# A scan block's residual: from an add on VectorE to a matmul on TensorE and a copy on ScalarE

## The chip, the cores and the metric

The kernel runs on one core of one Trainium2 chip. The metric is device time in microseconds (us): the median of the runs of one launch that computes the whole function.

## What is computed

The function is a chain of four blocks on x of shape (4, 512, 256), with a context of shape (4, 64, 192): a cross attention with a feed-forward part, a transformer block (self attention, cross attention, gated feed-forward part), four layers of a selective scan (Mamba), and a second transformer block. All is float32. The change lies in the scan layers:

```python
h = jnp.concatenate([p, x], axis=1)          # p: 64 tokens made of the context
for l in range(L_):                          # 4 layers
    h = h + mamba_block(rmsnorm(h, norm_w[l]), ...)

def mamba_block(x, ...):
    xi, z = split(einsum('bsd,ed->bse', x, ip_w))        # 512 channels each
    xi = silu(causal_conv4(xi) + cb)
    dt, Bm, Cm = split(einsum('bse,fe->bsf', xi, xp_w))
    dt = softplus(dt @ dtp_w.T + dtp_b)
    # for 16 states: state = exp(dt*A)*state + dt*B*xi ; y = sum(state*C)
    y = (ys + xi * Dp) * silu(z)
    return einsum('bse,de->bsd', y, op_w)                # the output projection
```

The residual is the `h +` of the loop: the output projection's result is added to h.

## The kernel before

The scan block is `layer2` (from line 1311). Its state `hT_res` holds h, transposed: 128 features on the partitions, in two chunks (DC = 2), for each of four batches 512 tokens. The work goes by **units**: a unit is one layer and one batch, 16 in all, in order. The 512 channels of a unit are four chunks of 128, treated as two pairs; for each pair there are 16 steps, so a unit has 32 steps, and a step carries two of the 16 states of one chunk.

The heart of a step i:

- **decay** (line 1636, ScalarE, recorded at line 1644): two exponentials of 128x512 into a PSUM tile `ps_dA`, of which there are two; it is issued one step ahead.
- **product** (line 1628, GpSimd, line 1632): `dBu` of 128x1022, issued two steps ahead; **begin** (line 1646) is a two-column copy by ScalarE into the same tile.
- **states** (line 1651, VectorE, line 1659): the scan over 128x1024, in place in `ps_dA`, or for every fourth step into the tile `hP`.
- **outputs_here** (VectorE, line 1666): the product with C into `hC`, for the three steps in four that did not go to `hP`; the fourth is multiplied by GpSimd (line 1670).
- **add_up** (line 1672, TensorE, line 1692): transposes of `hC` or `hP` that accumulate in the PSUM tile `ps_y`.

Beside these steps run generators, each of which issues a few instructions and yields; the loop (lines 1731 to 1797) advances all of them twice a step. The program's order is therefore written by the loop, and each engine runs its own instructions in that order. The generators are `front` (line 1368, normalisation, input projection, convolution and the x projection `ps_x` of a unit two ahead), `step` (line 1485, dt), `gate` (line 1527, the z projection: `ps_z`, copied to `zs` by ScalarE at line 1541), `gated` (line 1546, the end of a unit) and `tokens` (line 1578, the last layer's result turned back). They share two PSUM banks, taken and given back with `bank` and `done`; `need` makes a generator yield until one is free. At the 10th and 15th step of a unit `flush_silu` (line 1720) runs the pending SiLUs on ScalarE, with a table load before and one behind (lines 1723 and 1644).

`gated` runs for a pair two steps after the pair's last. For the second pair its work falls into the first steps of the next unit: it transposes the gated output `g` (line 1559), copies it to `gT` (ScalarE, line 1562), and then, for each feature chunk c of two, makes the output projection `ps_out` of four matmuls of 128x512 (by `in_halves`, line 174, which yields once in the middle; its matmuls are recorded at line 178), yields three times, and adds the residual on VectorE at line 1574. In the instruction order that add stands between a step's scan and its product with C.

Of the kernel before, what the change touches and what calls it, by code (L numbers as in the profile page):

```python
# [15 lines left out]
P = 128  # L16
# [12 lines left out]
EC = E // P  # L29
# [95 lines left out]
def kernel(ctx: ExitStack, tc: tile.TileContext, t: dict, out: bass.AP):  # L125
    nc = tc.nc

    keep = ctx.enter_context(tc.tile_pool(name="keep", bufs=1))
    ident = keep.tile([P, P], F32, name="ident")
# [20 lines left out]
    def load_w(pool, name, shape, p=P, src=None, **kw):  # L150
        w = pool.tile(shape, F32, name=f"w_{name}", **kw)
        nc.sync.dma_start(out=w, in_=(t[name] if src is None else src).rearrange("(c p) n -> p c n", p=p))
        return w
# [20 lines left out]
    def in_halves(dst, pairs):  # L174

        h = len(pairs) // 2
        for i, (l, r) in enumerate(pairs):
            nc.tensor.matmul(dst, l, r, start=(i == 0), stop=(i == len(pairs) - 1))  # L178
            if i == h - 1:
                yield  # L180
# [1116 lines left out]
    def load_l1(wp, n):  # L1297
        if n in ("Wk2", "Wv2"):
            return load_w(wp, f"L1_{n}", [CP, 2, FF], CP, tag="w8")
        if n in ("Wo1", "Wo2", "Wf"):  # L1300
            return load_w(wp, f"L1_{n}", [P, FF // P, D], tag="w8")
        if n in ("Wpa", "Wpg"):
            half = 0 if n == "Wpa" else FF
            return load_w(wp, f"L1_{n}", [P, DC, FF], src=t["L1_Wp"][:, half : half + FF], tag="w8")
        return load_w(wp, f"L1_{n}", [P, DC, FF], tag="w8")
# [5 lines left out]
    def layer2(hT, A, far, h63, tail, X, fw, wl, late):  # L1311
# [5 lines left out]
        with ExitStack() as st:  # L1317
# [14 lines left out]
            def bank(name="m"):  # L1332
                k = banks.pop(0)
                tl = psum.tile([P, T], F32, name=f"ps_{name}", tag=f"m{k}", bufs=1)
                held[id(tl)] = k, tl
                return tl
# [3 lines left out]
            def need(n, rank):  # L1340

                me = (rank, n)
                while len(banks) < n + sum(k for r, k in wants if r < rank):
                    if me not in wants:
                        wants.append(me)
                    yield
                if me in wants:
                    wants.remove(me)

            def done(*tiles):  # L1350
                banks.extend(held.pop(id(tl))[0] for tl in tiles)
# [194 lines left out]
            def gated(n, pair):  # L1546

                l, b = divmod(n, B)
                q = units[n]
                w, g, gT = q["w"], q["g"], q["gT"]  # L1550
                if b == 0 and pair == 0:
                    w["out"] = load_w(wl, "out", [P, EC, D], src=t["L2_out"][l], tag="out")
                yield
                yield
                for i in range(2):
                    yield from need(1, 2)
                    ps = bank("gt")
                    for j in range(TPB):
                        nc.tensor.transpose(ps[:, j * P : (j + 1) * P], g[:, j, i * P : (i + 1) * P], ident)
                    yield  # L1560
                    yield
                    nc.scalar.copy(gT[:, 2 * pair + i, :], ps)
                    done(ps)
                if pair == 0:
                    return
                for c in range(DC):
                    yield from need(1, 2)
                    ps = bank("out")
                    yield from in_halves(ps, [(w["out"][:, m, c * P : (c + 1) * P], gT[:, m, :]) for m in range(EC)])
                    yield  # L1570
                    yield
                    yield
                    h = hT[:, c, b, :]
                    nc.vector.tensor_add(h, ps, h)
                    done(ps)
                q["done"] = True

# [152 lines left out]
            with tc.manual_schedule():  # L1730
                for i in range(first, last):
# [42 lines left out]
                    if closing:  # L1774
                        en, er = divmod(e - 1, US)
                        close_pair(en, er // PS)
                        active.insert(0, gated(en, er // PS))
# [143 lines left out]
    hT = hT_pool.tile([P, DC, B, T], F32, name="hT_res")  # L1921
# [36 lines left out]
    with ExitStack() as st:  # L1958
# [6 lines left out]
        w = {n: load_l1(wp, n) for n in ("Wq1", "Wk1", "Wv1", "Wo1")}  # L1965
# [89 lines left out]
```

## Time and profile before

| | |
|---|---|
| median of 3 runs | 4092.45 us (4090.92 to 4098.35) |
| the profiled execution | 4095.76 us |
| its span (first to last instruction) | 4093.9 us |
| mean granted TensorE clock | 0.910 |
| busy over the span: TensorE matmul, VectorE, ScalarE, GpSimd | 85%, 74%, 52%, 58% |
| scans on VectorE (line 1659) | 512, 877.1 + 291.8 us |
| products with C on VectorE (line 1666) | 384, 469.7 us |
| decays on ScalarE (line 1644) | 1024, 708.0 us |
| residual adds on VectorE (line 1574) | 32, 0.691 us each (median) |

A row of the profile names a line, an engine (PE is TensorE's matmul, PEld its weight load, DVE VectorE, ACT ScalarE, POOL GpSimd, SP SyncE), an operation, output and inputs, and shapes. In a timeline the columns are start, duration, and the group; in square brackets stands the idle time of the engine just before, and what ended it. TensorE's matmuls are pipelined, so that a row's duration overlaps the next row's.

### The profile page before, as it was taken

How to read it: one execution, taken by the hardware profiler on the slowest of the kernel's cores; microseconds unless marked ns; L12 is line 12 of the kernel's file. 1: busy time of each engine (PE TensorE's matmuls, PEld its weight loads, DVE VectorE, ACT ScalarE, POOL GpSimd, SP SyncE). 2: the span in 40 equal slices, each digit the busy share in tenths (PEclk: the TensorE clock that was granted, in tenths of full speed). 3: DMA queues.
4: the chain of work that ended last, by engine and by line, in shares of the span. 5: the costliest groups of instructions: out<-in, count | busy, mean ns of one | idle time of the engine just before them, and what ended most of it. 6: DMA issues, size and time to landing. Idle time of an engine off the chain costs nothing. (4 is left out here: it accounts for less than half of the span.)

```text
span 4093.9 us, 48583 instructions
## 1 busy us (share of the span) xinstructions
PE 3488.9 (85%) x17616; PEld 2194.8 (54%) x17616; DVE 3034.5 (74%) x2903; ACT 2148.5 (52%) x4366; POOL 2384.8 (58%) x1625
## 2 busy tenths in 40 slices
PE   7989998998888897887888788888887667999889
PEld 4654554554566554555555555555555444555446
DVE  5538567466465643899999999999999996676653
ACT  2345455354322433666667666666666553556422
POOL 2339259077100424899999999999998881000131
PEclk8999999999989998888888888888888678999999
DMA  2023123023100102444444445444444431000000
GB/s 76 11 81 101 32 76 101 18 87 105 45 1 0 57 27 84 150 160 156 155 166 155 161 153 168 160 160 146 170 160 145 151 130 37 1 1 1 1 6 16
DMA packets 140287, 369.93 MB, mean 90 GB/s; under 512 B 20624, under 2 KB 38224, under 8 KB 140048
## 3 DMA queue, kind: packets, MB, share of 16 engines
q1 hardware_dynamic: 136688, 363.58, 26.6%
q10 hardware_dynamic: 3360, 3.25, 0.3%
q8 instruction: 139, 2.28, 0.2%
q14 instruction: 100, 0.82, 0.1%
HBM read 363.50 MB, written 3.28 MB: 90 GB/s over the span
## 5 line engine op out<-in xcount | busy, mean ns | idle before, releaser
L1632 POOL TENSOR_TENSOR dBu<-dtx,bB 128x1022 f32<-128x1022 f32 x512 | 1199.9, 2364 | 47.6 <-DVE ps_dA L1659 47.5
L1644 ACT ACTIVATE ps_dA<-dt,A 128x512 f32<-128x512 f32 x1024 | 708.0, 691 | 471.9 <-DVE hC L1666 405.0
L1659 DVE TENSOR_TENSOR_SCAN ps_dA<-ps_dA,dBu 128x1024 f32<-128x1024 f32 x384 | 877.1, 2284 | 37.1 <-ACT ps_dA L1644 28.9
L1692 PE MATMUL ps_y<-ident,hC 128*128 128x128 f32 x3072 | 443.3, 295 | 89.9 <-DVE hC L1666 89.9
L1666 DVE TENSOR_TENSOR hC<-ps_dA,bC 128x1024 f32<-128x1024 f32 x384 | 469.7, 1223 | 24.4
L1692 PEld LDWEIGHTS ps_y<-ident,hC 128*128 128x128 f32 x3072 | 388.3, 153 | 175.0 <-DVE hC L1666 120.3
L967 ACT ACTIVATE pr<-ps_s,nm 128x512 f32<-128x512 f32 x512 | 344.8, 685 | 260.4 <-DVE nm L963 260.3
L963 DVE TENSOR_REDUCE nm<-ps_s 128x2 f32<-128x1024 f32 x256 | 301.4, 1218 | 157.8 <-PE ps_s L952 143.4
L981 PE MATMUL ps_pt<-ident,pr 128*128 128x128 f32 x2048 | 284.6, 279 | 69.1 <-DVE pT L986 31.4
L1670 POOL TENSOR_TENSOR hP<-hP,bC 128x1024 f32<-128x1024 f32 x128 | 302.0, 2359 | 54.9 <-ACT dBu L1649 21.1
L1659 DVE TENSOR_TENSOR_SCAN hP<-ps_dA,dBu 128x1024 f32<-128x1024 f32 x128 | 291.8, 2280 | 53.9 <-POOL dBu L1632 49.2
L981 PEld LDWEIGHTS ps_pt<-ident,pr 128*128 128x128 f32 x2048 | 232.0, 142 | 167.1 <-issue 61.4
L616 POOL TENSOR_TENSOR ln_rstd<-ln_rstd,const 128x4 f32<-128x4 f32 x24 | 24.4, 1017 | 437.7 <-DVE ln_rstd L615 436.1
L178 PE MATMUL ps_cv<-xp,w_dg 128*128 128x512 f32 x512 | 244.7, 615 | 35.2 <-ACT dBu L1649 28.6
L535 DVE TENSOR_TENSOR_SCAN phb<-pdA,phb 128x512 f32<-128x512 f32 x128 | 225.7, 1779 | 60.9 <-POOL phb L525 44.8
L984 ACT COPY pT<-ps_pt 128x512 f32<-128x512 f32 x256 | 140.4, 592 | 173.1 <-PE ps_pt L981 172.5
L1000 PE MATMUL ps_o<-pT,V 128*64 128x256 f32 (+1 forms) x2048 | 222.8, 394 | 1.8 <-ACT AT L1018 1.8
L1692 PE MATMUL ps_y<-ident,hP 128*128 128x128 f32 x1024 | 167.0, 317 | 66.5 <-POOL hP L1670 66.5
L952 PE MATMUL ps_s<-kT,qT 64*128 64x512 f32 (+1 forms) x1024 | 209.0, 646 | 2.2 <-DVE kT L1172 1.3
L525 POOL TENSOR_TENSOR phb<-hT_res,pm 128x512 f32<-128x512 f32 x128 | 188.1, 1474 | 35.8 <-DMA pm<-scrp 22.2
L1692 PEld LDWEIGHTS ps_y<-ident,hP 128*128 128x128 f32 x1024 | 145.8, 167 | 113.7 <-POOL hP L1670 72.3
L784 POOL TENSOR_TENSOR pr<-pr,rs 128x512 f32<-128x512 f32 x64 | 65.3, 1042 | 228.5 <-DVE rs L782 210.3
(276 smaller groups left out, 6372.4 us busy)
## 6 DMA issues: line engine op xcount, KB each, us to landing
bB<-scr SPq DMA_DIRECT2D x256, 512.0 KB, 3.7
bC<-scr SPq DMA_DIRECT2D x256, 512.0 KB, 4.1
pm<-scrp SPq DMA_DIRECT2D x224, 256.0 KB, 3.2
w_pw_in<-in_L_in SPq DMA_DIRECT2D x7, 512.0 KB, 4.5
X<-in_x SPq DMA_DIRECT2D x4, 512.0 KB, 7.4
w_L_W<-in_L_W SPq DMA_DIRECT2D x2, 1024.0 KB, 9.9
w_L_Wq<-in_L_Wq SPq DMA_DIRECT2D x2, 1024.0 KB, 6.3
w_L_Wo<-in_L_Wo SPq DMA_DIRECT2D x2, 1024.0 KB, 8.7
```

Of the source, the lines that this page charges most:

```text
L178: nc.tensor.matmul(dst, l, r, start=(i == 0), stop=(i == len(pairs) - 1))
L535: nc.vector.tensor_tensor_scan(hb, dA, hb, 0.0, ALU.mult, ALU.add)
L963: nc.vector.tensor_reduce(nm, ps, AX.X, ALU.max, negate=True)
L967: nc.scalar.activation(pr, ps[:, x, :], AF.Exp, bias=nm[:, x : x + 1], accum_out=rs[:, y : y + 1])
L981: nc.tensor.transpose(pp[:, t4, :], pr[:, t4 * P : (t4 + 1) * P], ident)
L1000: nc.tensor.matmul(ps_o[0][j * stride : (j + 1) * stride, half * W2 : (half + 1) * W2], Vs[n][0][:, t4, h * stride : (h + 1) * stride], pT ...
L1632: nc.gpsimd.tensor_mul(dBu[:, :, 1:], dtx[:, 1:].unsqueeze(1).broadcast_to([P, 2, T - 1]), bmap[i // 2, 0][:, :, 1:])
L1644: nc.scalar.activation(dA, dt, AF.Exp, scale=A[:, l, m, s : s + 1])
L1659: nc.vector.tensor_tensor_scan(to, dA, dBus.pop(i).rearrange("p s t -> p (s t)"), 0.0, ALU.mult, ALU.add)
L1666: nc.vector.tensor_mul(hCs[i], dA, bmap[i // 2, 1])
L1670: nc.gpsimd.tensor_mul(hCs[i], hCs[i], bmap[i // 2, 1])
L1692: nc.tensor.matmul(y[:, j, k * P : (k + 1) * P], hC[:, s, j * P : (j + 1) * P], ident, is_transpose=True, start=False, stop=(2 * s2 + s == ...
```

## The change

For each chunk c the residual h becomes the first matmul of the output projection's group: the identity as the stationary operand and h as the moving one, accumulated in the same PSUM bank as the four weight matmuls. The add on VectorE is replaced by a plain copy from PSUM to h on ScalarE. The list that `in_halves` gets now has five pairs, so its yield comes behind the second matmul (identity and first weight matmul) and three follow it; of the three yields before the result is taken, one is dropped.

```diff
                 for c in range(DC):
                     yield from need(1, 2)
                     ps = bank("out")
-                    yield from in_halves(ps, [(w["out"][:, m, c * P : (c + 1) * P], gT[:, m, :]) for m in range(EC)])
-                    yield
-                    yield
-                    yield
                     h = hT[:, c, b, :]
-                    nc.vector.tensor_add(h, ps, h)
+                    yield from in_halves(
+                        ps, [(ident, h)] + [(w["out"][:, m, c * P : (c + 1) * P], gT[:, m, :]) for m in range(EC)]
+                    )
+                    yield
+                    yield
+                    nc.scalar.copy(h, ps)
                     done(ps)
                 q["done"] = True
```

More of the change, by code (lines that the diff above doesn't have):

```diff
@@ L1568, in gated @@
                     ps = bank("out")
-                    yield from in_halves(ps, [(w["out"][:, m, c * P : (c + 1) * P], gT[:, m, :]) for m in range(EC)])
+                    h = hT[:, c, b, :]
+                    yield from in_halves(
+                        ps, [(ident, h)] + [(w["out"][:, m, c * P : (c + 1) * P], gT[:, m, :]) for m in range(EC)]
+                    )
                     yield
                     yield
-                    yield
-                    h = hT[:, c, b, :]
-                    nc.vector.tensor_add(h, ps, h)
+                    nc.scalar.copy(h, ps)
                     done(ps)
```

## The prediction

> **What bounds the kernel now.** I read four views in this order. First the busy time by stretch: the change touches only the scan block (about 1605 to 3397 us), so its balance of engines counts, not the page's averages. This is the row of one stretch in it, with its headings:
>
> ```profile
> core 0: us, PE busy (x) PEld busy (x) DVE busy (x) ACT busy (x) POOL busy (x), PEclk, DMA share, GB/s
> 2000.00:2500.00 500.00, 417.43 (x1944) 281.74 (x1944) 480.85 (x291) 341.46 (x625) 471.96 (x287) 0.86 0.46 160
> ```
>
> VectorE is busy 96% there, ScalarE 68%, TensorE 83%. By shares alone, taking work off VectorE is right. Second, what is taken, from the answer on line 1574 (min/median/max ns, then what ended VectorE's wait before it):
>
> ```profile
> L1574 DVE TENSOR_TENSOR hT_res<-ps_out,hT_res x32: 672/691/693, 1753.4 to 3396.3; 128x512 f32<-128x512 f32 x32
> ...
>   PE ps_out L178: 14.8, 9
> ```
>
> Third, where VectorE's missing 4% lies. I listed every pause of VectorE over 0.15 us in the 15 units that start inside the loop. All have one in common, about 7 us after the second residual add of a unit: 1.2 to 2.0 us long, and 0.2 us in the last, where one SiLU runs instead of two. In a plain unit (period 108.0 us from second add to second add) it is the only one. Fourth, therefore, the timelines of the three engines around it. VectorE:
>
> ```profile
> 2081.86 0.67 DVE L1574 TENSOR_TENSOR hT_res<-ps_out,hT_res 128x512 f32<-128x512 f32 x1
> 2082.44 1.21 DVE L1666 TENSOR_TENSOR hC<-ps_dA,bC 128x1024 f32<-128x1024 f32 x1
> 2083.57 2.28 DVE L1659 TENSOR_TENSOR_SCAN hP<-ps_dA,dBu 128x1024 f32<-128x1024 f32 x1
> ...
> 2087.98 0.69 DVE L1574 TENSOR_TENSOR hT_res<-ps_out,hT_res 128x512 f32<-128x512 f32 x1
> ...
> 2095.26 2.30 DVE L1659 TENSOR_TENSOR_SCAN ps_dA<-ps_dA,dBu 128x1024 f32<-128x1024 f32 x1 [2.00 <-ACT ps_dA L1644]
> ```
>
> ScalarE over the same time:
>
> ```profile
> 2085.89 1.42 ACT L1644 ACTIVATE ps_dA<-dt,A 128x512 f32<-128x512 f32 x2 [0.67 <-DVE hP L1659]
> 2087.24 0.18 ACT L1649 COPY dBu<-h 128x2 f32<-128x2 f32 x1
> 2087.42 1.28 ACT L1723 ACT_TABLE_LOAD   x1
> 2088.71 1.92 ACT L1723 ACTIVATE xi<-xi 128x2048 f32<-128x2048 f32 x1
> 2090.53 1.89 ACT L1723 ACTIVATE zs<-zs 128x2048 f32<-128x2048 f32 x1
> 2092.45 1.28 ACT L1644 ACT_TABLE_LOAD   x1
> 2093.74 1.42 ACT L1644 ACTIVATE ps_dA<-dt,A 128x512 f32<-128x512 f32 x2
> ```
>
> From 2085.89 to 2095.16 ScalarE never rests: decays, table load, two SiLUs, table load, decays. The scan at 2095.26 starts 0.10 us after the last decay. So at this one place per unit ScalarE, not VectorE, sets the pace: whatever makes the SiLU block start later moves that scan by the same amount, and VectorE has no other pause in a plain unit in which to win it back. TensorE:
>
> ```profile
> 2075.72 1.88 PE L185 MATMUL ps_z<-w_inz,hn 128*128 128x512 f32 x4
> 2077.44 3.60 PE L178 MATMUL ps_out<-gT,w_out 128*128 128x512 f32 x8
> 2080.88 1.88 PE L185 MATMUL ps_z<-w_inz,hn 128*128 128x512 f32 x4
> 2082.59 1.04 PE L1692 MATMUL ps_y<-ident,hP 128*128 128x128 f32 x8
> 2083.47 1.04 PE L1692 MATMUL ps_y<-ident,hC 128*128 128x128 f32 x8
> 2084.34 3.60 PE L178 MATMUL ps_out<-gT,w_out 128*128 128x512 f32 x8
> 2087.78 1.91 PE L1692 MATMUL ps_y<-ident,hC 128*128 128x128 f32 x16
> ```
>
> No idle is noted on any of these rows: TensorE has a queue of work here and the second ps_out is ready at 2087.94, 0.04 us before VectorE takes it, and 0.52 us after ScalarE has already begun its SiLU block. The page's chain of waits starts only near 3401 us and says nothing of the scan.
>
> **The change, part by part.** The order of the two programs' instructions, compared per engine, shows: VectorE loses 32 adds and nothing else moves; GpSimd and SyncE (all DMA issues) are unchanged; TensorE gets 32 identity matmuls, and in each unit's second group the identity and the first weight matmul now stand ahead of the 16 ps_y transposes behind which all four weight matmuls stood; ScalarE gets 32 copies. Each copy stands one half step earlier than the add did: the first (c = 0) ahead of the decays that ran at 2079.78, the second (c = 1) ahead of the decays that ran at 2085.89.
>
> Removed: 32 x 0.691 = 22.1 us of VectorE, 30 of these in the loop. In a plain unit their time is given back to the 2.00 us pause, since the scan behind it waits for ScalarE; I count them at nothing there and carry them through the timeline below.
>
> Added on TensorE: a 128x512 f32 matmul is two rows in the trace, started 0.429 us apart (eight rows of a group from 2077.44 on), so an identity matmul is 0.86 us. Two come before the second group's end: +1.72 us, because the queue is full. [...]
>
> Added on ScalarE: the copy of a 128x512 f32 PSUM tile. The nearest row is the gT copy (line 1562), 0.58 us. The price is small; the wait is not. The copy waits for TensorE, and behind it in ScalarE's queue stand a dBu copy, two decays and the SiLU block. [...] The profile's order agrees so far (decays and copies start in program order everywhere), but no row here isolates a ready instruction that was passed or not. If it did pass, the copy would cost at most 0.58[...].
>
> Now one plain unit, in the times of these rows. First copy: ps_out ready at 2081.04 + 0.86 = 2081.90; copy to 2082.52; a 1-column copy, two decays (1.42) to 2083.97; the scan of 2083.57 starts at 2084.07, although without the add it could have started 0.6 earlier. Its successor's decays end by 2085.9, in time. Second copy: ps_out ready at 2087.94 + 1.72 = 2089.66; copy to 2090.28; decays to 2091.72; dBu copy; SiLU block from 2091.84 instead of 2087.42. From there the same 7.84 us to the scan: 2099.68 instead of 2095.26, **+4.42 us**. VectorE then pauses twice, about 2 us before the scan of 2089.72 and 4.4 us before this one.
>
> In general the block moves to 3.90 us after the old end of the second ps_out group. That old end lay 0.52 us after the old block start in nine units and 0.66 to 1.27 us in the six others (in these TensorE was already behind). So nine x 4.42 = 39.8, and six moves of 4.56, 5.17, 4.81, 5.17, 4.99 and 4.94 = 29.6: **69.4 us**. Cover elsewhere: TensorE, GpSimd and SyncE only move with it, as all they do next waits for the scan or for ScalarE. The last unit ends behind the loop: VectorE waits 7.72 and 2.74 us for its two groups, TensorE runs there at half clock in part, so one identity costs 1.7 and one 0.86, less 0.1 for a copy shorter than the add: **+2.5 us**. Sum 71.9.
>
> The unknown: the pause makes TensorE idle some 3.7 us before ps_x, where now it is idle 1.00 us. [...] the granted clock here is 0.66 in 2100 to 2130 and 1.00 in the 20 us after it[...]. At half clock the 8 ps_x rows take 3.4 us more, and ScalarE's xd copy waits for them; it now ends at 2097.18, 1.7 us before the next decays start. Whether and when the clock falls there is open; as its fall now comes at 2101, after ps_x, I take 0; the upper end is 3.4 - 1.7 = 1.7 us a unit, +26. [...]
>
> Base: the profiled execution took 4095.76 us (span 4093.9, 1.9 around it); + 71.9 = 4167.7. The median of the runs is 3.3 lower, 4092.45, so I state 4092.45 + 71.9 = **4164**.
>
> **The rivals.** *VectorE's relief (faster):* the 30 adds in the loop go off a 96% busy engine at 0.58 us a piece (add start to next start), -17.4; its waits for ps_out in the loop, 14.8 - 10.5 = 4.3, go too; + 2.5 at the end: 4073. It decides if the second ps_out stands ready when ScalarE reaches its copy, at 2085.2, 4.5 us before the 2089.66 worked out. For it speaks VectorE's 96%; against it the filled TensorE rows and the scan that waits for ScalarE. 5%. *TensorE has room:* the head-of-queue wait stays, the identities are free: 69.4 - 15 x 1.72 + 1 = +45, 4137. [...] against: no idle in the rows. 18%. *Half clock as well:* +1.7 us a unit on top, 4190. It decides if the clock falls before ps_x. For it: the longer pause[...]. 12%. *Nothing shows* (decays pass the copy, or pauses are regained): within 8 us of 4092; one pause a unit speaks against it. 4%.
>
> **How the numbers follow.** The main case has 61%, 4150 to 4178 by itself. From 4128 to 4188 I leave out the relief, no change, about half of the worst case and a little of the TensorE case: under 2 in 10. A measurement tells about 0.2% (8 us) from no change. Faster 0.05, same 0.04, slower 0.91.
>
> **What would show it.** Right: the copies (line 1575) wait nearly 4 us each for ps_out; the SiLU block of a plain unit starts about 3.9 us after what used to be the group's end; the pause before the scan behind it grows from 2.0 to over 4 us and a new one of about 2 us stands one scan ahead; the period grows from 108.0 to 112.4 us; VectorE's busy time falls by 22 us while the span grows. Wrong: if copies hardly wait, the TensorE sum has failed; if they wait but the scan does not move, decays ran ahead of them or had slack I missed.

## The result, and the profile after

The changed kernel takes 4163.55 us (median of 4 runs, 4161.81 to 4166.52), the kernel before 4092.95 us (4 runs): 70.6 us or 1.7% slower, ratio 1.0170 with a 95% interval of 1.0154 to 1.0186. The forecast was 4164.

ScalarE after the change, the same place in a plain unit (two copies of this unit, and what is queued behind the second; the bracket is idle time and what ended it):

```profile
2089.87 0.59 ACT L1575 COPY hT_res<-ps_out 128x512 f32<-128x512 f32 x1 [3.61 <-PE ps_out L178]
...
2097.63 0.59 ACT L1575 COPY hT_res<-ps_out 128x512 f32<-128x512 f32 x1 [3.84 <-PE ps_out L178]
2098.11 0.20 ACT L1650 COPY dBu<-h 128x2 f32<-128x2 f32 x1
2098.20 1.42 ACT L1645 ACTIVATE ps_dA<-dt,A 128x512 f32<-128x512 f32 x2
2099.56 0.18 ACT L1650 COPY dBu<-h 128x2 f32<-128x2 f32 x1
2099.74 1.28 ACT L1724 ACT_TABLE_LOAD   x1
```

Both copies wait nearly 4 us for TensorE, and the decays, then the SiLU block, start in a row as soon as the second copy is through. VectorE in the same stretch, its three scans that had to wait:

```profile
2091.97 2.29 DVE L1660 TENSOR_TENSOR_SCAN hP<-ps_dA,dBu 128x1024 f32<-128x1024 f32 x1 [0.76 <-ACT ps_dA L1645]
...
2099.73 2.30 DVE L1660 TENSOR_TENSOR_SCAN ps_dA<-ps_dA,dBu 128x1024 f32<-128x1024 f32 x1 [1.97 <-ACT ps_dA L1645]
...
2107.57 2.30 DVE L1660 TENSOR_TENSOR_SCAN ps_dA<-ps_dA,dBu 128x1024 f32<-128x1024 f32 x1 [4.23 <-ACT ps_dA L1645]
```

Where one pause of 2.00 us stood there are three, 6.96 us together, all ended by decays. A ready instruction was held: the decays of 2098.20 write the `ps_dA` tile that the hP scan of 2091.97 gave back when it ended near 2094.3 (before, the same decays started as soon as that scan released them: the row of 2085.89 in the prediction), and they ran 3.9 us later, right behind the copy. TensorE:

```profile
2091.39 1.02 PE L178 MATMUL ps_out<-hT_res,ident 128*128 128x512 f32 x2
2092.25 1.02 PE L178 MATMUL ps_out<-gT,w_out 128*128 128x512 f32 x2
...
2094.85 2.74 PE L178 MATMUL ps_out<-gT,w_out 128*128 128x512 f32 x6
2097.43 1.91 PE L1693 MATMUL ps_y<-ident,hC 128*128 128x128 f32 x16
2103.00 5.33 PE L178 MATMUL ps_x<-xi,w_xp 128*48 128x512 f32 x8 [3.66 <-ACT xi L1724]
```

The identity's two rows take 0.86 us from start to next start (their 1.02 us overlap the next row by 0.16), and no idle stands on the rows before ps_x: TensorE is as full as it was. The 32 copies' waits by sum (line 1575, then what ended the idle before it: us, times):

```profile
L1575 ACT COPY hT_res<-ps_out x32: 586/587/593, 1748.6 to 3459.0; 128x512 f32<-128x512 f32 x32
...
  PE ps_out L178: 120.5, 32
```

Before, VectorE waited 14.8 us in all for the same tiles, 9 times. Where the time came from, by the two profiled executions (4095.76 and 4162.62 us, 66.9 apart): from the first scan to the last 1771.3 us became 1838.5, +67.2; ahead of the first scan it was 5.3 less, from the start of the last scan on 4.9 more. I count these two as spread, but for 0.7 us: apart from the last unit's two groups the program is the same there, and over the nine profiles of this study, seven of them of other kernels, the first scan starts between 1598 and 1607 us and the stretch from the start of the last one on takes 715.7 to 720.6 us.

### The profile page after: what moved, and what is told of

Its sections match the earlier page's. It is cut to its first block, busy times and chain, and to the rows that moved or that the text cites. A ratio compares the mean times of both kernels' runs of the same rounds, so it can differ in the third digit from the quotient of the medians.

```text
span 4160.8 us, 48722 instructions
## 1 busy us (share of the span) xinstructions
PE 3547.5 (85%) x17680; PEld 2212.7 (53%) x17680; DVE 3021.1 (73%) x2871; ACT 2161.9 (52%) x4398; POOL 2385.8 (57%) x1625
## 3 DMA queue, kind: packets, MB, share of 16 engines
q8 instruction: 140, 2.29, 0.2%
## 5 line engine op out<-in xcount | busy, mean ns | idle before, releaser
L1633 POOL TENSOR_TENSOR dBu<-dtx,bB 128x1022 f32<-128x1022 f32 x512 | 1200.4, 2363 | 107.6 <-DVE ps_dA L1660 107.5
L1693 PE MATMUL ps_y<-ident,hC 128*128 128x128 f32 x3072 | 452.9, 299 | 66.0 <-DVE hC L1667 66.0
```

Source lines behind the costliest of these rows:

```text
L1633: nc.gpsimd.tensor_mul(dBu[:, :, 1:], dtx[:, 1:].unsqueeze(1).broadcast_to([P, 2, T - 1]), bmap[i // 2, 0][:, :, 1:])
L1693: nc.tensor.matmul(y[:, j, k * P : (k + 1) * P], hC[:, s, j * P : (j + 1) * P], ident, is_transpose=True, start=False, stop=(2 * s2 + s == ...
```

## The experiments

The theory: the copy waits at the head of ScalarE's queue for a TensorE that is full, the decays and the SiLU block wait behind it, and each scan behind those waits as long. The rivals: the identity matmuls' 27 us of TensorE are the cost themselves; or ScalarE's added copies are; or VectorE's busy time is what counts. The table has the plain unit's period (the shortest, where like units differ) and the time from the first scan's start to the last one's in each profile, both in us; the ratios are to the kernel before on the same chip.

| kernel | median us | ratio (95%) | plain unit | first to last scan |
|---|---|---|---|---|
| before | 4092.95 | | 108.0 | 1771.3 |
| after | 4163.55 | 1.0170 (1.0154 to 1.0186) | 112.4 | 1838.5 |
| e1 identity, copy on VectorE | 4099.45 | 1.0015 (1.0009 to 1.0022) | 108.1 | 1777.9 |
| e2 copy on ScalarE, no identity | 4139.52 | 1.0113 (1.0098 to 1.0129) | 110.7 | 1814.9 |
| e4 copies later | 4105.07 | 1.0030 (1.0021 to 1.0038) | 108.3 | 1780.7 |
| e6 adds later, VectorE | 4111.58 | 1.0050 (1.0037 to 1.0063) | 109.4 | 1789.3 |
| e3 SiLU block a step later | 4173.84 | 1.0191 (1.0177 to 1.0205) | 113.4 | 1850.6 |
| e5 no add at all | 4089.02 | 0.9992 (0.9984 to 1.0000) | 107.6 | 1767.8 |
| e7 adds later, earlier than e6 | 4090.27 | 0.9989 (0.9982 to 0.9995) | 107.6 | 1767.6 |

For e1, e2, e4 and e6 the kernel before had a median of 4092.77 us, for e3, e5 and e7 of 4094.29 us.

### The identity alone (e1)

```diff
                     yield
                     yield
-                    nc.scalar.copy(h, ps)
+                    yield
+                    nc.vector.tensor_copy(h, ps)
                     done(ps)
```

> The identity matmuls stay, but the copy goes to VectorE, at the place of the old add (three yields again). Theory (a copy that waits at the head of ScalarE's queue holds back the decays and the SiLU block): ScalarE's queue is as before, so the SiLU block stays; VectorE waits some 1.6 us for the second ps_out, which the pause of 2.0 us behind it takes up; the end of the block costs 2.5 us: 4092 to 4100. Rival (the 32 identity matmuls themselves are the cost, 0.86 us each on a full TensorE): +27, about 4120.

Measured: 4099.45, at the upper end. VectorE's second copy and the scan behind the SiLU block, then the waits of all 32 copies:

```profile
2087.73 0.69 DVE L1576 COPY hT_res<-ps_out 128x512 f32<-128x512 f32 x1 [1.55 <-PE ps_out L178]
...
2093.40 2.30 DVE L1661 TENSOR_TENSOR_SCAN ps_dA<-ps_dA,dBu 128x1024 f32<-128x1024 f32 x1 [0.39 <-ACT dBu L1651]
```

```profile
  PE ps_out L178: 38.3, 24
```

VectorE waits 1.55 us for the longer group, and the pause behind shrinks from 2.00 to 0.39 by about as much. Its waits for ps_out grew by 23.5 us in all (14.8 before), close to the identities' 27, and yet the kernel lost only 6.7: the wait is covered as long as the engine that waits has a pause coming. The rival that TensorE's work is the cost falls. The 6.7 us are not where they were expected, at the end of the block: between the first and the last scan 6.6 us were added, 1.9 of them in the last unit, whose pause of 0.2 us had nothing to give.

### The copy alone (e2)

```diff
-                        ps, [(ident, h)] + [(w["out"][:, m, c * P : (c + 1) * P], gT[:, m, :]) for m in range(EC)]
+                        ps, [(w["out"][:, m, c * P : (c + 1) * P], gT[:, m, :]) for m in range(EC)]
```

> The copy on ScalarE stays where the change put it, without the identity matmul: the residual is left out of the result. Theory: the second ps_out is ready 1.72 us earlier and nothing else changes, so the loss falls from 69.4 by 15 x 1.72 to 43.6 and the end of the block costs nothing: 4136. Rival (the identity matmuls are the cost): back at 4092. Rival (the wait costs nothing by itself, only the copies' 0.58 us on ScalarE): 15 x 1.2 = 18, 4110.

Measured: 4139.52; the scan block grew by 43.6 us, as worked out. Line 1575's waits here:

```profile
  PE ps_out L178: 92.7, 32
```

So the wait at the head of ScalarE's queue alone is some 44 to 47 of the 70 us, and the identities make up the rest by lengthening that wait (120.5 - 92.7 = 27.8, about 32 x 0.86). The whole is more than its parts: the identity alone costs 6.7, the copy alone 46.8, both 70.6. The identity is dear only where ScalarE waits for it.

### The copies behind what they blocked (e4)

```diff
-                    yield
-                    yield
+                    for _ in range(5):
+                        yield
                     nc.scalar.copy(h, ps)
```

> All of the change stays, but there are five yields ahead of the copy instead of two, so that the first copy stands behind the next decays and the second behind the SiLU block. Theory: no copy waits long. The identity still delays the last ps_z and so its copy zs and the decays behind it; with the first copy's own 0.58 us the SiLU block starts about 0.5 us later: 15 x 0.5 + 2.5 = 10, about 4102. Rival (it is TensorE's added work or ScalarE's added copies, wherever they stand): still 4150 to 4165.

Measured: 4105.07. ScalarE, then VectorE:

```profile
2080.58 0.58 ACT L1575 COPY hT_res<-ps_out 128x512 f32<-128x512 f32 x1
...
2082.68 1.28 ACT L1724 ACT_TABLE_LOAD   x1
...
2091.77 0.58 ACT L1575 COPY hT_res<-ps_out 128x512 f32<-128x512 f32 x1
```

```profile
2080.73 2.30 DVE L1660 TENSOR_TENSOR_SCAN ps_dA<-ps_dA,dBu 128x1024 f32<-128x1024 f32 x1 [0.38 <-ACT ps_dA L1645]
...
2090.51 2.30 DVE L1660 TENSOR_TENSOR_SCAN ps_dA<-ps_dA,dBu 128x1024 f32<-128x1024 f32 x1 [2.65 <-ACT ps_dA L1645]
```

No bracket stands on either copy: the same work on the same engines, three half steps later in the queue, gives back 58 of 70 us. Of all experiments this one comes closest to isolating the cause: identities and copies are all there, and what differs is the copies' place in the queue. The second group's matmuls move with it: they start behind 24 ps_y transposes, where 16 had stood in the middle of the group, so its result comes later by 1.4 us from the unit's start, and not earlier. VectorE gains nothing from the adds it lost: its pauses here, 2.65 and 0.38 us, are 1.03 us longer than the one of 2.00, more than the two adds had taken from its time (0.42 us each, see below), and the period is 0.3 us above that of before.

### The adds in VectorE's pause (e6), and one step earlier (e7)

The edit of e6; e7 has `range(3)` instead of `range(5)`. The call of `in_halves` is shortened.

```diff
+                outs = []
                 for c in range(DC):
                     yield from need(1, 2)
                     ps = bank("out")
+                    outs.append(ps)
                     yield from in_halves(ps, ...)
                     yield
-                    yield
-                    yield
+                for _ in range(5):
+                    yield
+                for c, ps in enumerate(outs):
                     h = hT[:, c, b, :]
                     nc.vector.tensor_add(h, ps, h)
```

> The kernel before, with the add on VectorE and no identity; both output groups are issued first, and both adds stand behind the SiLU block's decays' step, in VectorE's 2.0 us pause. Theory: the adds (2 x 0.69) fit into the pause, the scan that releases the decays ahead of the SiLU block comes 0.57 us earlier, so the block does too: 15 x 0.57 + 4.3 of waits for ps_out = 13 faster, 4080, at most 4092. Rival (VectorE's busy time is what counts): no change, since it does the same work.

Measured: 4111.58, so the expectation failed. The pause did shrink, to 1.19 us, and came 0.4 us earlier, but each plain unit got a new one of 1.78 us some 32 us later. Holding both PSUM banks for longer had moved the front on: its ps_x matmuls now wait for the adds (38.1 us, 11 times, where before none did) and start 36.5 us into a plain unit instead of 33.9, and the dt stage comes later with them. Who waits for the adds, then ScalarE in the dt stage:

```profile
  PE ps_x L178: 38.1, 11
```

```profile
2118.00 0.69 ACT L1500 ACTIVATE dt<-ps_dt,cols 128x512 f32<-128x512 f32 x1 [2.41 <-PE ps_dt L1498]
2118.71 1.28 ACT L1309 ACT_TABLE_LOAD   x1
...
2122.45 1.42 ACT L1647 ACTIVATE ps_dA<-dt,A 128x512 f32<-128x512 f32 x2
```

It is the same pattern at another place: a ScalarE instruction that waits for TensorE, a table load behind it, decays behind that. The scan at 2123.97 waits for those.

> The kernel before with both adds issued one step earlier than in the first late try, ahead of the scan before the pause; with this the instruction order of TensorE, ScalarE and SyncE is that of the kernel before, and only the adds move on VectorE. Theory: the SiLU block comes 0.4 us earlier a unit, its pause takes up the adds, and nothing collides later: 15 x 0.4 + 4.3 = 10 faster, 4082. Rival (late adds cost by themselves, as the 19 us of the first try could be read): 4100 to 4112.

Measured: 4090.27 against 4094.29 on the same chip, faster by 0.11% (interval 0.05 to 0.18%): it beats both kernels, but by 4 us and not the 10 expected. VectorE, the adds and the pause that is left:

```profile
2085.34 1.28 DVE L1577 TENSOR_TENSOR hT_res<-ps_out,hT_res 128x512 f32<-128x512 f32 x2
...
2091.32 2.30 DVE L1662 TENSOR_TENSOR_SCAN ps_dA<-ps_dA,dBu 128x1024 f32<-128x1024 f32 x1 [1.24 <-ACT ps_dA L1647]
```

The period fell by the 0.4 us that was expected. What did not come are the 4.3 us of VectorE's waits for ps_out in the units where TensorE is behind: there other pauses grew or appeared (in one such unit a scan waits 1.65 us instead of 0.95, in another a new pause of 1.09 us stands).

### No add at all (e5)

```diff
                     h = hT[:, c, b, :]
-                    nc.vector.tensor_add(h, ps, h)
                     done(ps)
```

> The kernel before without the residual add (h is never updated, so both the residual and the block's output are left out there); the output projections still run. It bounds what taking the adds off VectorE can bring. Theory: the SiLU block sets the pace, so the 1.38 us a unit only lengthen the pause in front of the scan behind it, but for the 0.4 us that the scan ahead of the block comes earlier (its decays wait for the zs copy otherwise): 15 x 0.4 + 4.3 of waits for ps_out in the loop = 10, about 4082. Rival (VectorE's relief): 30 x 0.58 + 4.3 = 22 and more, 4071.

Measured: 4089.02 against 4094.29, where 4082 was expected; the interval of the ratio reaches 1.0000. The period is that of e7, and the pause has grown to 2.38 us. All of the 22 us that VectorE spends on the residual are worth about 4 us (3.5 between the first and the last scan, 5.3 between the medians). In this order of instructions that is about what the change could have won, had its copies cost nothing.

### The SiLU block a step later (e3)

```diff
-                    if main and r in (10, 15):
+                    if main and r in (11, 15):
```

> All of the change stays, but the SiLU block comes one step later (at the 11th step instead of the 10th), so that one more pair of decays stands between the second copy and it. Theory: the copies hold back the decays as before (pauses of 0.76 and about 2 us), but VectorE has work from one more step before it needs what stands behind the block: the pause there is about 2.4 instead of 4.24 us. 15 x (0.76 + 1.96 + 2.4 - 2.0 - 1.38) = 26, + 2.5: about 4122, at most 4132. Rival (TensorE's added work or the copies' own time is what counts, wherever the block stands): 4163.

Measured: 4173.84, slower than the changed kernel, so the expectation failed. VectorE, the scan behind the SiLU block and a later one:

```profile
2116.76 2.29 DVE L1660 TENSOR_TENSOR_SCAN hP<-ps_dA,dBu 128x1024 f32<-128x1024 f32 x1 [2.14 <-ACT ps_dA L1645]
...
2146.51 2.29 DVE L1660 TENSOR_TENSOR_SCAN hP<-ps_dA,dBu 128x1024 f32<-128x1024 f32 x1 [3.15 <-ACT ps_dA L1645]
```

Behind the block the pause is 2.14 us instead of 4.23, near the 2.4 worked out. The second is new, and again it is the dt stage of the next unit. It moved with the block, since the front's ps_x matmuls wait for the SiLU (the bracket on ps_x above), and line 1500 now stands behind one more pair of decays:

```profile
2140.54 0.69 ACT L1500 ACTIVATE dt<-ps_dt,cols 128x512 f32<-128x512 f32 x1 [2.16 <-PE ps_dt L1498]
2141.25 1.28 ACT L1309 ACT_TABLE_LOAD   x1
```

Line 1500 waits 51.5 us for TensorE in this kernel, 12.5 us in the kernel before and 13.9 us in the changed one. So this run does not tell the theory from its rival by its time; by its pauses it fits the theory.

## Why the prediction was right

*What bounds the kernel.* Right: ScalarE sets the pace at one place a unit. e5 shows it from the other side, since VectorE's adds can go without a gain of more than about 4 us.

*The second copy.* The SiLU block was to start 2.18 us after the group's new end (3.90 after the old one); it starts 2.15 us after it in each of the 15 units. The copies were to wait nearly 4 us; they wait 3.61 and 3.84. The scan behind the block was to pause 4.4 and the one ahead of it about 2 us; they pause 4.23 and 1.97. The period was to grow to 112.4; it is 112.39. The third pause, 0.76 us behind the first copy, lies in the prediction's own timeline (the scan that starts at 2084.07) but not in its count of two.

*The rows on TensorE's room.* The rows were right: e2 takes the identities away and the time falls by 24 us, near the 15 x 1.72 = 26 that the prediction takes off for free identities. That TensorE has room for one more matmul at this place was the assumption of the rival *TensorE has room*; it was not shown by any row, and it does not hold here. e1 does not speak for it either: TensorE had no room there, but the engine that waited had a pause.

*Ready decays behind the copy.* That they would not pass it was assumed in the sum, without a row that showed it. It is shown by the rows of 2097.63 and 2098.20 and by e4: decays whose tile was free near 2094.3 did not pass the copy and started 3.9 us later, and with the copies later in the queue 58 of 70 us came back.

*The sum.* 69.4 us for the loop; the profiles say 67.2. The terms for the six units in which TensorE was behind were too large: 29.6 us in all were given, and the scans behind the block moved by 4.09 to 4.74 us in these units, 26.1 in all. In the other nine they moved by 40.7 us, for 39.8 given. Why the six fell short is not shown. The last unit was put at +2.5 us; from the start of the last scan to the end of the last copy it is 19.4 us where it was 18.7 to the end of the last add, so +0.7: only the first identity ran at half clock there (1.87 us; granted 0.50 in 3448 to 3450), while most rows of weight matmuls behind it ran at full clock (granted 0.66 in 3450 to 3452 and 1.00 in 3452 to 3460; before, the first of them had run at half: granted 0.50 in 3386 to 3390). Between the two profiles the change cost 66.9 us, 5 less than the 71.9 forecast; that the medians lie 70.6 apart, and the forecast within 1 us of the median, is luck. The term of a plain unit is not.

*The half clock.* The zero was right, but not for the reason given. The clock does fall at ps_x: in the 3.66 us of idle time ahead of it the granted clock was still 1.00 (2101 to 2103), in its first 2.5 us it was 0.52 (2103.0 to 2105.5), and the eight rows took 5.33 us instead of 3.63, 5.0 to 5.3 us in all 14 units of the loop. That is 1.70 us more in this unit, where the slow case had put 3.4, an estimate that doubles eight rows of 0.429 us. It cost nothing because the xd copy stands behind four decays in ScalarE's queue: before, it started 2.29 us after ps_x was done, and now 0.59. The sum for the slow case had left this room out. The same idle time did not always go with slow rows: in e2 it was 3.66 us too, and ps_x still took 3.63 us in 4 of the 14 units. What decides it is not shown.

*VectorE's busy time* fell by 13.4 us (3034.5 to 3021.1), not by 22. An add between a scan and its product with C had cost less than its row. A scan with its product, first before, with the add between, then after:

```profile
2085.77 2.27 DVE L1659 TENSOR_TENSOR_SCAN ps_dA<-ps_dA,dBu 128x1024 f32<-128x1024 f32 x1
2087.98 0.69 DVE L1574 TENSOR_TENSOR hT_res<-ps_out,hT_res 128x512 f32<-128x512 f32 x1
2088.59 1.21 DVE L1666 TENSOR_TENSOR hC<-ps_dA,bC 128x1024 f32<-128x1024 f32 x1
```

```profile
2087.59 2.29 DVE L1660 TENSOR_TENSOR_SCAN ps_dA<-ps_dA,dBu 128x1024 f32<-128x1024 f32 x1
2089.98 1.23 DVE L1667 TENSOR_TENSOR hC<-ps_dA,bC 128x1024 f32<-128x1024 f32 x1
```

Without the add the product starts 0.1 us after the scan's end; with it each row overlaps the next by about 0.08 us. From the scan's start to the product's the median is 2.79 us with an add that did not wait and 2.36 without, so an add took 0.42 us of VectorE's time, and not the 0.58 of the prediction's rival or the 0.6 of its timeline. The 0.4 us by which the block came earlier in e6 and e7, where 0.57 had been expected in e6, fits this.

## What to carry to other kernels

Before an eviction moves to another engine, ask what stands behind it in that engine's queue and when its input will be ready, not what it costs: here two copies of 0.59 us each waited nearly 4 us, and decays whose tile had been free for those 4 us started only behind the second. An engine with 32% idle time (ScalarE, busy 341 of 500 us before) can still set the pace at one point of a period, and a bound engine's relief is worth only what the next pause doesn't take (e5: 22 us of adds were worth about 4). The same pattern (an instruction that waits for TensorE, with a table load behind it) came back at another place in two of the four reordered kernels (e3 and e6), so after a reordering the new pauses are to be looked for over the whole period.

## What had not been expected of the hardware

The dt matmuls in the middle of a unit often take nearly twice their time (two rows 2.07 us instead of 1.12), and whether this costs anything depends on when ScalarE comes for them. The changed kernel, TensorE and the ScalarE instruction that takes the result, and then TensorE in e6:

```profile
2126.28 2.07 PE L1498 MATMUL ps_dt<-xd,w_dt 16*128 16x512 f32 x2
2128.39 0.69 ACT L1500 ACTIVATE dt<-ps_dt,cols 128x512 f32<-128x512 f32 x1
```

```profile
2115.90 2.07 PE L1498 MATMUL ps_dt<-xd,w_dt 16*128 16x512 f32 x2
```

The granted clock around all three groups (this one, e6's, and e3's of 2138.43) was 0.50, and two rows took 2.07 us, where a group of the kernel before (at 2109.19) took 1.12 us at a granted clock of 1.00. Before, the second group of the stage took 2.07 us in 13 of 15 units, after the change in 14. In these two kernels ScalarE is busy with decays until the group is done or nearly so, and no wait stands on the row of 2128.39. In e3 and e6 it comes to line 1500 while the group is still running, waits 2.16 and 2.41 us, and the group's 2.07 us at the granted 0.50 lie within that wait. How much of it the clock alone makes was not measured.
